# A graph layer on one core: preparation in a hand-written order, the output's bias loaded by type, and an input of the last norm added by TensorE

## The chip, the cores and the metric

The kernel runs on one core of a Trainium2 chip. The metric is the device time of one execution in microseconds; the times below are from three runs, and one further execution was profiled. The engines are named as in the profile: PE (TensorE, the matmuls; PEld its weight loads), DVE (VectorE), ACT (ScalarE), POOL (GpSimd, which also issues the gathers and scatters by index), SP (SyncE, which issues most plain transfers).

## The reference, cut to what matters

One layer of a graph network over N = 3125 nodes of width 256, E = 103125 edges (sorted by destination) and 19 node types. All in float32.

```python
h = layernorm(x)                                   # per row
# graph part: projections with the matrices of the node's own type; four heads of 56
K, Q, V = h @ Wk[type] + bk[type], h @ Wq[type] + bq[type], h @ Wv[type] + bv[type]
e0, e1, e2 = (cos(log(edge_attr[:, i] + 1)[:, None] * w_time + b_time) for i in range(3))
# each edge gives a message from src to dst and one back; q is summed over its heads
att, v = messages(K[src], Q[dst], V[src], e1, e2);  att_i, v_i = messages(K[dst], Q[src], V[dst], e2, e1)
agg = segment_sum([v * segment_softmax(att, dst), e0], dst) + segment_sum([v_i * segment_softmax(att_i, src), e0], src)
y = layernorm(h + concat(agg, agg) @ Wa[type] + ba[type]) * gamma[type] + beta[type]
# mixing part: linear attention over all nodes, 8 heads, phi(u) = elu(u) + 1
k, v, q = phi(h @ wk + bk), h @ wv + bv, phi(h @ wq + bq)
m = (q @ (k.T @ v)) / (q @ sum(k) + 1e-6) @ wo + bo       # per head
X = x + y + m
# mixture of 16 experts, two for each node, and a last norm
z = layernorm(X)
out = X + layernorm(z + experts(z)) * gamma2 + beta2
```

(The kernel sums the two halves of `Wa`, which meet the same `agg`.)

## The kernel before, in words

Rows of 128 nodes make a tile: NT = 25 tiles in the order of the nodes, JS = 43 tiles in the order of the types (a tile has one type, `owner_s[j]`), JT = 64 tiles in the order of the experts.

**Preparation (L193 to L593).** The node tiles lie in `XN`; their norm is taken (bn_stats L424, bn_aggr L425, normalise L430), each tile is transposed into `XNT` (L285, L286) and scattered by type to `xbuf` in memory. For the edges, `dst` is read as `idx` and turned to floats (`nf`); 25 counts over `firsts` (L391) give `row_i`, the line in which each node's edges begin, 25 gathers `er` and 25 counts (L401) the place within it. The nodes are sorted by type (`sorted_rows`) and by number of edges: the degree sort (L468 to L494) makes running sums of 25 x 64 one-hot entries, ranks by matmul (`pr`, L487, L488), and at the end `place_i`. 25 scatters put the node records into `order`, and `ordt` is read back from it (L555). The edge attributes are brought to logarithms in four quarters (L507 to L517, written to `recs`). The weights `w` hold Wk and Wv as they are, and Wq folded from 192 to 56 columns (`fold`, L527 to L529), one type at a time with two buffers. The mixing part's sums over nodes are made in a loop over 25 tiles: keys and values by matmul (`ps_kv`, L573), `k`, `low`, `v` and again `k` by VectorE (L576, L578, L581, L583, with the exponential on ScalarE), and the sum over rows by matmul (`acc`, L585); then `state`. In all of this stage a scheduler decides each engine's order.

**Projection (L716 on, order by hand).** Per type tile: `xr` from `xbuf` and `bias` from `bbuf` by SP (the bias is one row, repeated over 128 partitions; the row's number is loaded into a register first), two transposes, a matmul with the type's weights (L726), `prow` (L734, three buffers), and a scatter of it into `table` (L740) by POOL. The queries and the mixing part of the node tiles, the sums of the two halves of Wa (L753) and, from the ninth tile on, the edge lists (which need `ordt`) are worked in between.

**Edge blocks.** 25 blocks of gathers from `table` and the attention; from 519 to 2038 us of the span. The change does not touch them.

**Output (L916 on, order by hand).** In groups of four type tiles (QUAD): `ar` (the edge sums) and `yr` (the rows of `xbuf`) are loaded two groups ahead by SP, `ar` is transposed one group ahead, and per tile PE adds up three products in `ps_yo`: the bias (L967), which is the type's row picked out of `ba` by a one-hot matrix, and two halves of the weights (L970). VectorE adds the result to `yr` (L974) and takes the moments; one group later ScalarE normalises and POOL scatters the rows to `obuf`. Between the tiles POOL gathers scale rows `Z` and VectorE adds to `X`.

```python
ps = ps_out.tile([P, D], F32, name="ps_yo")
nc.tensor.matmul(ps, sel_s[:, j:j + 1].to_broadcast([T, P]), ba, start=True, stop=False)
```

**Experts and last norm.** After the experts, `ybuf` holds two result rows for each node. They are fetched in parts of LN = 3 tiles (`yb`), PE adds the two by a product with the identity (L1204), VectorE adds the sum to `Z` (L1225), takes the moments (L913, L914), ScalarE normalises from `Z` (L1210), VectorE multiplies by gamma and adds `X` (L1211, L1212), and SP writes the output. Parts are fetched three ahead and summed one ahead.

Of the kernel before, what the change touches and what calls it, by code (L numbers as in the profile page):

```python
# [97 lines left out]
def gnn_mix_moe_kernel(ctx: ExitStack, tc: tile.TileContext, a, out):  # L98
# [97 lines left out]
    e2 = right.enter_context(tc.tile_pool(name="eprep2", bufs=2, side="right"))  # L196
# [19 lines left out]
    turned = first.enter_context(tc.tile_pool(name="turned", bufs=1))  # L216
    normed = ExitStack()
# [18 lines left out]
    for i, k in enumerate(("wq", "wk", "wv")):  # L236
        nc.sync.dma_start(wqkv[:, :, i, :], a[f"L0_mix_{k}"].rearrange("(c p) o -> p c o", p=P))
    wo = mw.tile([P, 2, D], F32, name="wo")
    nc.sync.dma_start(wo, a["L0_mix_wo"].rearrange("(c p) o -> p c o", p=P))
# [7 lines left out]
    nc.vector.tensor_scalar(bq1, bqc, 1.0, None, op0=OP.add)  # L247
# [8 lines left out]

    zp = first.enter_context(tc.tile_pool(name="zero", bufs=1))
    none = ep.tile([P, ROW], F32, name="none")
    nc.gpsimd.memset(none, -1.0)
# [3 lines left out]
    scales = zp.tile([T, 2, DZ], F32, name="scales")  # L263
# [4 lines left out]
    bo = zp.tile([T, D], F32, name="bo")  # L268
    src = a["L0_mix_bo"]
    nc.gpsimd.dma_start(bo, bass.AP(tensor=src.tensor, offset=src.offset, ap=[[0, T], [1, D]]))  # L270
    nc.vector.tensor_tensor(scales[:, 1, :D], scales[:, 1, :D], bo, OP.add)
# [4 lines left out]

    wp = first.enter_context(tc.tile_pool(name="wproj", bufs=1))
    w = wp.tile([P, T, 2, WC], F32, name="w")
# [17 lines left out]

    def sorted_rows(gp, ps_r, pick, K, J):

# [7 lines left out]
        nc.tensor.matmul(total.rearrange("p t e -> p (t e)"), ones, pv, start=True, stop=True)  # L306
        run = gp.tile([P, NT + 1, K], F32, name="run0")
# [59 lines left out]

    nf = ep.tile([P, EW + 1], F32, name="nf")
    nc.vector.tensor_copy(nf, idx)
    kept_ends = nc.gpsimd.dma_start(ends.rearrange("(p r) t -> p (r t)", p=P), nf[:, :EW]).ins  # L370
    with tc.issue_after(kept_ends):
        nc.sync.dma_start(xbuf.rearrange("(t p) d -> p t d", p=P), bc(blank, 1, JS + 1))
    down = ep.tile([P, EW], F32, name="down")
    nc.vector.tensor_tensor(down, nf[:, :EW], nf[:, 1:], OP.is_gt)
    nc.vector.tensor_reduce(bad[:, 0:1], down, AX.X, OP.max)


    ps = ps_c.tile([P, LR, P], F32, name="ps_first")
    for r in range(LR):
        nc.tensor.transpose(ps[:, r, :], nf[:, r * ET:r * ET + 1].to_broadcast([P, P]), ident)  # L380
    firsts = ep.tile([P, LR * P], F32, name="firsts")
    nc.scalar.copy(firsts, ps.rearrange("p r q -> p (r q)"))
    node_i = ep.tile([P, NT], I32, name="node_i")
    nc.gpsimd.iota(node_i, pattern=[[P, NT]], base=0, channel_multiplier=1)
    rec = ep.tile([P, NT, 4], F32, name="rec")
    node = rec[:, :, 0]
    nc.vector.tensor_copy(node, node_i)
    row = ep.tile([P, NT], F32, name="row")
    for t in range(NT):
        junk = e2.tile([P, max(ET, LR * P)], F32, name="junk", bufs=1)  # L390
        nc.vector.tensor_scalar(junk[:, :LR * P], firsts, node[:, t:t + 1], 0.0, op0=OP.is_lt, op1=OP.add,  # L391
                                accum_out=row[:, t:t + 1])
    nc.vector.tensor_scalar(row, row, -1.0, 0.0, op0=OP.add, op1=OP.max)
    row_i = ep.tile([P, NT], I32, name="row_i")
    nc.vector.tensor_copy(row_i, row)
    within = ep.tile([P, NT], F32, name="within")
    for t in range(NT):
        er = e2.tile([P, ET], F32, name="er", bufs=6)
        counted = gather_rows(er, ends, row_i[:, t:t + 1]).ins
        junk = e2.tile([P, max(ET, LR * P)], F32, name="junk", bufs=1)  # L400
        nc.vector.tensor_scalar(junk[:, :ET], er, node[:, t:t + 1], 0.0, op0=OP.is_lt, op1=OP.add,  # L401
                                accum_out=within[:, t:t + 1])


    with tc.tile_pool(name="sort", bufs=1) as gp, tc.tile_pool(name="ps_r", bufs=1, space=PSUM) as ps_r:
        type_f = gp.tile([P, NT], F32, name="type_f")
        nc.vector.tensor_copy(type_f, type_p)
        nc.vector.tensor_scalar(gtype, type_f, 0.0, None, op0=OP.max)
        pick = gp.tile([P, NT, T], F32, name="pick")
        nc.vector.tensor_tensor(pick, bc(type_f, 2, T), bc(seq[:, :T], 1, NT), OP.is_equal)  # L410
        base, own = sorted_rows(gp, ps_r, pick, T, JS)
        row_of(gp, pick, base, T, JS * P, stype_f)
        nc.vector.tensor_copy(stype, stype_f)
        nc.vector.tensor_copy(owner_s, own[0:1, :])
        nc.vector.tensor_scalar(sel_s, own[:T, :], pcol[:T], None, op0=OP.is_equal)


    mv = stats.tile([P, NT, 2], F32, name="mv_x")
    rs = stats.tile([P, NT], F32, name="r_x")
    with tc.tile_pool(name="ps_t", bufs=2, space=PSUM) as ps_t:  # L420
        for g0, gn in groups:
            for t in range(g0, g0 + gn):
                st = stats.tile([P, nc.vector.BN_STATS_DIM], F32, name="s_x", bufs=4)
                nc.vector.bn_stats(st, XN[:, t, :D])  # L424
                nc.vector.bn_aggr(mv[:, t, :], st)  # L425
            gs = slice(g0, g0 + gn)
            nc.scalar.activation(rs[:, gs], mv[:, gs, 1], AF.Sqrt, bias=eps_c)
            nc.vector.reciprocal(rs[:, gs], rs[:, gs])
            for t in range(g0, g0 + gn):
                nc.vector.tensor_scalar(XN[:, t, :D], XN[:, t, :D], mv[:, t, 0:1], rs[:, t:t + 1],  # L430
                                        op0=OP.subtract, op1=OP.mult)
                transposed(XNT[:, :, t * P:(t + 1) * P], XN[:, t, :D], ps_t, "pt")
                with tc.issue_after(counted):
                    scatter_rows(xbuf, stype[:, t:t + 1], XN[:, t, :], "xrows")


    start = ep.tile([P, NT + 1], F32, name="start")
    nc.vector.memset(start[:, NT:], 0.0)
    nc.vector.scalar_tensor_tensor(start[:, :NT], row, float(ET), within, op0=OP.mult, op1=OP.add)
    nc.vector.tensor_copy(rec[:, :, 1], start[:, :NT])  # L440

    shift = ep.tile([P, 2, P], F32, name="shift")
    nc.vector.memset(shift, 0.0)
    nc.vector.tensor_copy(shift[:, 0, :P - 1], ident[:, 1:])
    nc.vector.tensor_copy(shift[:, 1, P - 1:], ident[:, 0:1])
    ps = ps_c.tile([P, NT], F32, name="ps_next")
    nc.tensor.matmul(ps, shift[:, 0, :], start[:, :NT], start=True, stop=False)
    nc.tensor.matmul(ps, shift[:, 1, :], start[:, 1:], start=False, stop=True)
    deg = ep.tile([P, NT], F32, name="deg")
    nc.vector.tensor_tensor(deg, ps, start[:, :NT], OP.subtract)  # L450
    if NP > N:
        nc.vector.tensor_scalar(deg[:, FULL:], deg[:, FULL:], live, None, op0=OP.mult)
# [115 lines left out]
    for v in vs:  # L568
        nc.vector.memset(v[:, :, P:], 1.0)
# [1163 lines left out]
```

## Time and profile before

| | us |
|---|---|
| median of three runs (2707.68 to 2709.11) | 2709.07 |
| the profiled execution: time | 2717.76 |
| the profiled execution: span | 2716.0 |
| PE busy (share of the span) | 2084.6 (77%) |
| DVE busy | 1918.1 (71%) |
| POOL busy | 1497.5 (55%) |
| ACT busy | 1230.2 (45%) |
| mean granted clock of PE | 0.839 |

How to read it: the span runs from the first to the last instruction of the profiled execution, and all places in time below are microseconds from its start. Busy shares are means over stages that have different limits. The granted clock is the share of full speed at which PE was allowed to run; it was 0.50 or 1.00 in most stretches. A line such as "L726 PE MATMUL ps<-w,xT" names the line of the kernel, the engine, the operation, and the tiles that it writes and reads; "x25 | 10.1, 406 | 9.3 <-PE ps_yy L1204" stands for 25 instructions, 10.1 us busy, 406 ns each, and 9.3 us in which the engine stood idle before them, released by PE's `ps_yy` of L1204.

### The profile page before, as it was taken

The numbers are of one execution on the slowest core, as the hardware profiler recorded it, in microseconds if no ns is written. First come the engines' busy times: TensorE is split into PE (matmuls) and PEld (weight loads), VectorE is DVE, ScalarE is ACT, GpSimd is POOL, SyncE is SP. The second block draws the span as 40 slices with busy tenths as digits, with TensorE's granted clock in tenths as the row PEclk, the third lists the DMA queues.
The fourth block names the chain that finished last, engine by engine and source line by source line (L and its number), as shares of the span: only waits on it lengthen the run. The fifth ranks groups of instructions, "written<-read, shape, count | busy, mean of one in ns | idle before, by whom it ended". The sixth has DMA issues, their size and how long they took to land. (4 is left out here: it accounts for less than half of the span.)

```text
span 2716.0 us, 28309 instructions
## 1 busy us (share of the span) xinstructions
PE 2084.6 (77%) x7139; PEld 1274.6 (47%) x7139; DVE 1918.1 (71%) x3769; ACT 1230.2 (45%) x3019; POOL 1497.5 (55%) x1525
## 2 busy tenths in 40 slices
PE   2268665278898898989988888898877853599994
PEld 1034342134555455555554554455554541377773
DVE  7465777377889899999999998999972463122226
ACT  1112222265666666666666566657632350133332
POOL 3531468776777777777777776766613614222210
PEclk7579787677989898999899899898986755699997
DMA  9434567896667666666666766666636561255554
GB/s 282 137 77 129 165 194 226 286 314 183 181 202 202 177 192 192 195 197 193 190 198 202 199 187 178 192 182 188 178 124 204 174 197 66 99 174 173 174 156 146
DMA packets 236151, 496.03 MB, mean 183 GB/s; under 512 B 31509, under 2 KB 148340, under 8 KB 235476
## 3 DMA queue, kind: packets, MB, share of 16 engines
q0 software_dynamic: 88480, 325.71, 40.2%
q1 hardware_dynamic: 139428, 158.87, 20.0%
q10 hardware_dynamic: 8080, 9.59, 1.2%
q8 instruction: 63, 1.03, 0.1%
q14 instruction: 100, 0.82, 0.1%
HBM read 415.68 MB, written 78.37 MB: 182 GB/s over the span
## 5 line engine op out<-in xcount | busy, mean ns | idle before, releaser
L357 POOL DMA_INDIRECT rowt<-table,idx x854 | 999.8, 1171 | 394.6 <-issue 231.3
L1394 PE MATMUL pl<-rowt,ident 128*128 128x448 f32 (+2 forms) x944 | 496.9, 681 | 100.5 <-issue 55.3
L1394 PEld LDWEIGHTS pl<-rowt,ident 128*128 128x128 f32 x944 | 210.3, 234 | 382.2 <-issue 283.8
L1446 PE MATMUL pa<-keep,ident 128*128 128x256 f32 x1708 | 380.6, 380 | 7.0 <-DVE keep L1444 7.0
L1446 PEld LDWEIGHTS pa<-keep,ident 128*128 128x128 f32 x1708 | 325.7, 191 | 73.5 <-issue 27.7
L1359 PE MATMUL ps_u<-wide,turned 49*128 49x448 f32 (+2 forms) x708 | 323.2, 592 | 47.9 <-ACT turned L1352 27.0
L1338 DVE TENSOR_TENSOR rowt<-rowt 128x1260 f32<-128x1260 f32 (+2 forms) x118 | 178.4, 1512 | 140.4 <-DMA rowt<-table,idx 61.7
L1328 ACT ACTIVATE rowt<-rowt,KT 128x60 f32<-128x60 f32 x854 | 216.2, 334 | 20.9 <-DMA rowt<-table,idx 20.0
L1359 PEld LDWEIGHTS ps_u<-wide,turned 49*128 49x128 f32 x708 | 128.0, 194 | 189.7 <-issue 126.0
L351 POOL DMA_INDIRECT ybuf<-y,to_i x64 | 61.4, 960 | 265.0 <-DVE y L1169 224.0
L1352 ACT COPY turned<-pt 42x128 f32<-42x128 f32 (+2 forms) x118 | 30.6, 259 | 386.6 <-PE pt L1350 218.3
L1387 DVE TENSOR_TENSOR rowt<-rowt,qq 128x672 f32<-128x672 f32 (+2 forms) x236 | 197.7, 878 | 4.0
L1361 ACT ACTIVATE half<-ps_u 128x448 f32<-128x448 f32 (+2 forms) x354 | 190.9, 539 | 2.2 <-remote 1.1
L1161 ACT ACTIVATE hT<-ps_h,b 128x128 f32<-128x128 f32 x256 | 94.1, 368 | 213.2 <-PE ps_h L1160 211.5
L1160 PE MATMUL ps_h<-zT,w 128*128 128x128 f32 x1024 | 180.1, 295 | 12.6 <-ACT hT L1161 10.0
L1339 DVE TENSOR_REDUCE KT<-rowt 128x21 f32<-128x1260 f32 (+2 forms) x118 | 178.3, 1511 | 4.1
L1160 PEld LDWEIGHTS ps_h<-zT,w 128*128 128x128 f32 x1024 | 149.8, 192 | 58.2 <-ACT hT L1161 44.0
L1440 DVE TENSOR_TENSOR keep<-keep,both 128x1176 f32<-128x1176 f32 (+2 forms) x118 | 167.0, 1416 | 0.0
L1355 ACT COPY keep<-rowt 128x1344 f32<-128x1344 f32 (+2 forms) x118 | 159.1, 1348 | 13.3 <-PE pa L1446 13.3
L1165 PE MATMUL ps_e<-w,hT 128*128 x512 | 157.6, 390 | 0.0
L1373 PE MATMUL pe<-te,ident 128*128 128x256 f32 x472 | 117.1, 371 | 34.9 <-ACT te L1362 24.4
L1362 ACT ACTIVATE te<-half 128x448 f32<-128x448 f32 (+2 forms) x236 | 139.1, 590 | 7.8 <-ACT half L1361 0.3
(374 smaller groups left out, 3375.6 us busy)
## 6 DMA issues: line engine op xcount, KB each, us to landing
w<-in_L_ffn_w_dram SPq DMA_DIRECT2D x80, 512.0 KB
rowt<-table,idx POOLq DMA_INDIRECT x854
h<-in_L_gnn_Wa_dram SPq DMA_DIRECT2D x19, 512.0 KB
bias<-bbuf SPq DMA_DIRECT2D x43, 220.0 KB
zbuf<-zero SPq DMA_DIRECT2D x1, 8514.0 KB
zr<-zbuf SPq DMA_DIRECT2D x64, 129.0 KB
yb<-ybuf SPq DMA_DIRECT2D x16, 384.0 KB
xbuf<-blank SPq DMA_DIRECT2D x1, 5654.0 KB
```

Of the source, the lines that this page charges most:

```text
L357: return nc.gpsimd.indirect_dma_start(out=dst, out_offset=None, in_=buf[:, :], in_offset=IndirectOffsetOnAxis(ap=idx, axis=0))
L1160: nc.tensor.matmul(ps[:, f, :], w1[:, c, f * P:(f + 1) * P], zT[:, c, :], start=(c == 0), stop=(c == 1))
L1328: nc.scalar.activation(key[:, s, :], key[:, s, :], AF.Square, bias=chk[q]["b"]["k"][:, s0 + s, 1:2])
L1338: nc.vector.tensor_tensor(times, times, bc(rowt[:, :n, :CAP], 2, 3), OP.mult)
L1339: nc.vector.tensor_reduce(b["times"][:, s0:s1, 1::2], times, AX.X, OP.add)
L1355: nc.scalar.copy(keep[:, :n, :PROJ], rowt[:, :n, VC:QC])
L1359: nc.tensor.matmul(ps[:, :n * 2 * TD], lT, wide[:, k, :n * 2 * TD], start=True, stop=True)
L1361: nc.scalar.activation(half[:, :n, :].rearrange("p s j -> p (s j)"), ps[:, :n * 2 * TD], AF.Sin)
L1387: nc.vector.tensor_tensor(to, kt, bc(qq[:, :n, d, :], 2, 3), OP.mult)
L1394: nc.tensor.matmul(pl[:, :n], ident, part[:, :, :, a, :], start=(a == 0), stop=(a == PARTS - 1))
L1440: nc.vector.tensor_tensor(v3, v3, bc(b["both"][:, s0:s1, :3], 3, DK), OP.mult)
L1446: nc.tensor.matmul(b["pa"], ident, keep[:, s, :], start=(s0 + s == 0), stop=(s0 + s == c - 1))
```

## The change

Three edits, in one version.

First, everything from the edges' first counts to `state` stands in one `manual_schedule` block, in which each engine's order is that of the text. SP asks for the mixing weights, the blank of `xbuf`, Wk and Wv ahead of everything else; ScalarE loads the last two edge quarters. The 25 edge counts run in one piece ahead of the type sort; all moments are taken before one square root. A loop over the 25 tiles normalises, transposes and counts, with a key tile (`keys`: the products and VectorE's part for one tile, and the sum of the tile before) behind every second one; the scatters to `xbuf` come behind the loop. The degree sort is a generator (`order_rows`) with 14 steps, behind each of which one `keys()` runs, and every third time one of five folds (four types each instead of one). The scatters to `order` follow, each with a copy of its index column by POOL ahead (`apart`), as do those to `xbuf`.

Second, the output's bias row is loaded by type for each tile (`bas`) and added to `yr` by VectorE (`shift`); the product with `sel_s` goes.

Third, in the last norm `Z` enters the sum on PE as a third product with the identity; the moments and ScalarE read the sum in PSUM. Parts have two tiles instead of three, are fetched four ahead and summed two ahead, with more buffers.

The diff, cut to its core:

```diff
-    ba = wp.tile([T, D], F32, name="ba")
-    nc.scalar.dma_start(ba, a["L0_gnn_ba"])
...
+            bas[j] = op.tile([P, D], F32, name="ba", bufs=2 * QUAD)
+            ks = nc.sync.value_load(owner_s[0:1, j:j + 1], min_val=0, max_val=T - 1)
+            nc.sync.dma_start(bas[j], a["L0_gnn_ba"][bass.ds(ks, 1), :].to_broadcast([P, D]))
+
+        def shift(j):
+            y = yrs[j][:, :D]
+            nc.vector.tensor_tensor(y, y, bas.pop(j), OP.add)
...
             for j in parts[i + 1]:
                 turn(j)
+            for j in range(j0, j1):
+                shift(j)
             if i > 0:
                 write(*groups[i - 1])
             for j in range(j0, j1):
                 kp = nc.tensor.value_load(owner_s[0:1, j:j + 1], min_val=0, max_val=T - 1)
                 ps = ps_out.tile([P, D], F32, name="ps_yo")
-                nc.tensor.matmul(ps, sel_s[:, j:j + 1].to_broadcast([T, P]), ba, start=True, stop=False)
                 agT = agTs.pop(j)
                 for c in range(2):
                     nc.tensor.matmul(ps, agT[:, c, :],
                                      wa[:, bass.ds(kp, 1), c * D:(c + 1) * D].rearrange("p t o -> p (t o)"),
-                                     start=False, stop=(c == 1))
+                                     start=(c == 0), stop=(c == 1))
...
-        with tc.tile_pool(name="fin", bufs=4) as fo, tc.tile_pool(name="ps_fin", bufs=6, space=PSUM) as ps_fin:
+        with tc.tile_pool(name="fin", bufs=6) as fo, tc.tile_pool(name="ps_fin", bufs=8, space=PSUM) as ps_fin:
-            LN = 3
+            LN = 2
...
-                        ps = sums[t] = ps_fin.tile([P, D], F32, name="ps_yy")
+                        ps = sums[t] = ps2[:, t - t0, :]
+                        nc.tensor.matmul(ps, ident, Z[:, t, 0, :D], start=True, stop=False)
                         for k in range(2):
-                            nc.tensor.matmul(ps, ident, ybs[i][:, k, t - t0, :], start=(k == 0), stop=(k == 1))
+                            nc.tensor.matmul(ps, ident, ybs[i][:, k, t - t0, :], start=False, stop=(k == 1))
...
-                        nc.scalar.activation(y, Z[:, t, 0, :D], AF.Identity, bias=ms[:, t:t + 1], scale=rs[:, t:t + 1])
+                        nc.scalar.activation(y, sums.pop(t), AF.Identity, bias=ms[:, t:t + 1], scale=rs[:, t:t + 1])
...
-                        z = Z[:, t, 0, :D]
-                        nc.vector.tensor_tensor(z, z, sums.pop(t), OP.add)
-                        moments(mv, t, z, "f")
+                        moments(mv, t, sums[t], "f")
```

The new order of the preparation, with what it calls (added lines of the diff):

```python
def apart(idx, side):
    at = ep.tile([P, 1], I32, name=f"at_{side}", bufs=3)
    nc.gpsimd.tensor_copy(at, idx)
    return at
...
with tc.manual_schedule():
    ...
    for q in range(2):
        load_edges(q, nc.sync)
    for i, k in enumerate(("wq", "wk", "wv")):
        nc.sync.dma_start(wqkv[:, :, i, :], a[f"L0_mix_{k}"].rearrange("(c p) o -> p c o", p=P))
    nc.sync.dma_start(wo, a["L0_mix_wo"].rearrange("(c p) o -> p c o", p=P))
    nc.sync.dma_start(xbuf.rearrange("(t p) d -> p t d", p=P), bc(blank, 1, JS + 1))
    load_w(w[:, :, :, :PROJ], a["L0_gnn_Wk"], nc.sync)
    load_w(w[:, :, :, PROJ:2 * PROJ], a["L0_gnn_Wv"], nc.sync)
    ...
    def keys():
        t = n_keys[0]
        n_keys[0] += 1
        if t < NTR:
            keys_of(t)        # ps_kv, k, low, v
        if 0 < t <= NTR:
            sum_keys(t - 1)   # the second k, acc

    keep_edges(0)
    load_edges(2, nc.scalar)
    keep_edges(1)
    load_edges(3, nc.scalar)
    with tc.tile_pool(name="ps_t", bufs=2, space=PSUM, side="right") as ps_t:
        for t in range(NT):
            if t + 6 < NT:
                kept_er[t + 6] = er_p.tile([P, ET], F32, name="er")
                gather_rows(kept_er[t + 6], ends, row_i[:, t + 6:t + 7])
            nc.vector.tensor_scalar(XN[:, t, :D], XN[:, t, :D], mv[:, t, 0:1], rs[:, t:t + 1],
                                    op0=OP.subtract, op1=OP.mult)
            transposed(XNT[:, :, t * P:(t + 1) * P], XN[:, t, :D], ps_t, "pt")
            junk = er_p.tile([P, max(ET, LR * P)], F32, name="junk", bufs=1)
            nc.vector.tensor_scalar(junk[:, :ET], kept_er.pop(t), node[:, t:t + 1], 0.0, op0=OP.is_lt, op1=OP.add,
                                    accum_out=within[:, t:t + 1])
            if t % 2 == 1 and t > 2:
                keys()
    for t in range(NT):
        scatter_rows(xbuf, apart(stype[:, t:t + 1], "x"), XN[:, t, :], "xrows")
    ...
    for q in range(2, 4):
        keep_edges(q)
    ...
    for i in range(2):
        load_fold(i)
    ...
    steps = order_rows()
    i = 0
    for s, _ in enumerate(steps):
        if n_keys[0] <= NTR:
            keys()
        if s % 3 == 2 and i < len(folds):
            fold_one(i)
            i += 1
    for t in range(NT):
        scatter_rows(order, apart(place_i[:, t:t + 1], "o"), rec[:, t, :], "order")
    nc.gpsimd.dma_start(ordt, order.rearrange("(t p) c -> p t c", p=P))
    while n_keys[0] <= NTR:
        keys()
    while i < len(folds):
        fold_one(i)
        i += 1
    ...
```

## The prediction

> **What bounds the kernel now.** The page comes first: no engine is full for the whole span. Its two rows of 40 slices (68 us each) show where the changed stages lie: slices 1 to 4 (preparation, then the start of the projection loop), 31 and 32 (output projection behind the edges), and the last one (final norm). The edge blocks between them are untouched.
>
> ```profile
> DVE  7465777377889899999999998999972463122226
> PEclk7579787677989898999899899898986755699997
> ```
>
> Second, the windows, one per stage, for busy time and granted clock (columns: window, length, PE busy, PEld, DVE, ACT, POOL, clock, DMA share, GB/s).
>
> ```profile
> 116.00:147.00 31.00, 13.59 (x16) 4.85 (x17) 24.49 (x71) 6.75 (x11) 2.05 (x3) 0.50 0.41 127
> 147.00:228.00 81.00, 60.12 (x199) 30.55 (x197) 45.41 (x153) 9.58 (x23) 26.34 (x26) 0.89 0.28 58
> 2056.00:2086.00 30.00, 29.95 (x68) 17.63 (x68) 9.56 (x30) 6.07 (x15) 6.71 (x10) 0.50 0.59 180
> 2086.00:2120.00 34.00, 32.15 (x135) 20.22 (x134) 17.03 (x54) 13.17 (x33) 23.03 (x35) 1.00 0.88 269
> 2661.00:2693.00 32.00, 24.37 (x92) 18.17 (x91) 29.29 (x94) 9.70 (x21) 1.41 (x2) 0.92 0.61 206
> ```
>
> The reader sees that from 147 to 228, where 23 of the 25 key tiles run, VectorE is busy 56% of the time; in the output stage TensorE is full at first, at half clock; in the final norm VectorE is full (92%).
>
> Third, the timeline: the two rows that decide when POOL is free, one key tile in the present steady state, and a row of the projection (start, length, what).
>
> ```profile
> 186.16 0.97 POOL L351 DMA_INDIRECT order<-rec,place_i  x1 [0.30 <-issue]
> 190.54 1.62 POOL L555 DMA_DIRECT2D ordt<-order  x1 [3.42 <-issue]
> ...
> 203.10 0.42 DVE L576 TENSOR_TENSOR k<-ps_kv,bkv 128x256 f32<-128x256 f32 x1 [0.25 <-PE ps_kv L573]
> 203.45 1.88 PE L573 MATMUL ps_kv<-wqkv,XNT 128*128 128x512 f32 x4
> 204.60 0.43 DVE L583 SCALAR_TENSOR_TENSOR k<-k,low 128x256 f32<-128x256 f32 x1 [0.54 <-ACT low L579]
> 205.17 0.62 PE L585 MATMUL acc<-v,k 128*128 128x129 f32 x4
> ...
> 252.97 0.62 DVE L734 TENSOR_TENSOR prow<-ps,bias 128x440 f32<-128x440 f32 x1
> ```
>
> `place_i` is written at 154.8, the order scatters run 155 to 187, POOL is free at 192.2; the first table scatter starts at 240.6. So 48 us of slack lie between them. The keys' end (228) and the queries, not the order list, set the projection's start at 237.4. The fourth row of the projection table is made at 252.97.
>
> Fourth, the groups of the two last stages:
>
> ```profile
> L970 PE MATMUL ps_yo<-wa,agT 128*128 x172 | 64.6, 511 | 0.0
> L351 POOL DMA_INDIRECT obuf<-yo,to x43 | 43.0, 999 | 54.1 <-ACT yo L942 41.3 <-issue 8.8 <-POOL to L944 3.5
> L967 PE MATMUL ps_yo<-ba,sel_s 19*128 19x256 f32 x86 | 38.1, 530 | 4.9 <-DVE yr L974 2.9 <-issue 1.9
> ...
> L1204 PE MATMUL ps_yy<-yb,ident 128*128 128x256 f32 x100 | 29.0, 446 | 15.1 <-DVE Z L1225 8.0 <-DMA yb<-ybuf 6.7
> L1225 DVE TENSOR_TENSOR Z<-Z,ps_yy 128x256 f32<-128x256 f32 x25 | 10.1, 406 | 9.3 <-PE ps_yy L1204 9.3
> ```
>
> **Part 1, the hand order.** I follow the one chain that ends in the order list.
>
> Start of the loop over XN: in the new order ScalarE's loads of the edge quarters 2 and 3 stand behind the loads of Wk and Wv (the compiled program has them wait for the lanes of these transfers), and VectorE's `keep_edges(1)` behind those. About 18.6 MB are asked for before that: x 3.2, dst 0.4, edges 1.2, mix weights 1.0, xbuf's blank 5.8, Wk 3.7, half of Wv 1.9, gathers and fills 1.4. Slice 1 moved 282 GB/s: 66 us, and some 6 for a late start, the Ln (1.76) and the reduction (0.77): the loop starts at 72. VectorE's own work before it (25 edge counts of 0.82, 25 moments of 0.6, the type sort of 12) would end at about 63 and hides behind the loads.
>
> The loop: 11 rounds of two tiles and one key tile. In TensorE's order a round is acc 0.71, two transposed tiles 1.06, kv 1.88, together 3.65; then VectorE needs k, low, v and the second k, 1.53, before the next acc; with 0.2 of handing over 5.4 us, at half clock 7.3+1.7 = 9.0. Today a key tile costs 2.2, because the scheduler puts kv ahead of the acc that waits. One round at half clock and ten at full are 63, the four tiles without keys 4: end at 139. `keep_edges` 2 and 3 (0.34, 1.76, 0.77 each and one table load of 1.28) take 7: 146.
>
> The order sort: 14 steps, each followed by one `keys()`. Its own VectorE work (running sums of 1.5 to 2.0, three ranks of 2.0) hides behind acc and kv; a round is 0.71+1.88+1.53+0.2 = 4.3, at half clock 7.0. The four pairs of rank matmuls (a full one 1.9) stand ahead of kv and add 6. I take four rounds at half clock, since TensorE has just been idle for 7 us, and ten at full: 28+43+6 = 77. `place_i` comes at 223 instead of 155.
>
> Then POOL: each order scatter now has its index copy ahead, as L944 has before the scatters of the output (0.20+0.28+0.98 = 1.47): 25 take 36.8, and the ordt transfer 5.0 (3.42 idle, 1.62). The table scatters are queued behind it on POOL; `prow` has three buffers, so the fourth waits for the first scatter (copy and issue 1.5, landing estimated at 2). 223+45.3 = 268.3 against 252.97: **+15.3**. The other path, over the last key, fold, state, checks and queries (some 15.5 from `place_i` to the first product, 9 of them as now between 228 and 237.4; then 15.5 to the fourth row, as now from 237.4 to 252.97), would give 254, so it is hidden. The five larger folds instead of 19 save some 6 us of VectorE, beside waits; they are worth nothing here, and would count only if the loop were VectorE's. The xbuf scatters (25 of 1.47, done by about 155) hide under the order sort. No engine is full in the projection loop (TensorE 12.5 of 20 us, VectorE 13.6), but its tiles follow each other in order, so I pass the delay on whole.
>
> Ends: all rounds at full clock and the loads done 6 us earlier put `place_i` at 202 and the term at -6; half of the loop and all of the order rounds at half clock give +40.
>
> A page bears on this: the Trainium skill, "TensorE: Matmul & The Clock Gate", section "What's actually happening", says that full clock comes after one window of about 3.4 us of sustained activity. By that rule one half-clock round is enough after the pause, and the term is about +7, not +15. The row 2056 to 2086 speaks against it: busy 29.95 of 30 us, clock 0.50. By that row, seven half-clock rounds, it would be +23. Four lies between.
>
> **Part 2, the bias by type.** Removed: 43 L967, 38.1 us of TensorE. Added per tile: a register load and a broadcast transfer on SP, and a VectorE addition of 0.42 (18 us in all, beside VectorE at 32 to 50%). In the projection loop the same pair follows an xr load at 1.6 us a tile; with ar and yr (0.95 together) I get 2.15 a tile, 8.6 a group of four. TensorE at half clock needs 4 x 2.01 + 1.71 = 9.75 a group instead of 14.35; POOL 4 x 1.47 + 2 x 1.29 = 8.5. So all three come close to each other. The second group's transposes stand ahead of the first product, so that it waits for eight tiles' loads: 2043.4+17.2+2+1.7 = 2064 instead of 2056.7; the four products then take 8 instead of 12.6, and the first scatter comes at 2076 instead of 2073.5. From it POOL needs 94 us (43 x 1.47 and 24 x 1.29), with 0 to 10 us of gaps (today 14): end at 2170 to 2180 against 2181.7. I take **-6**; ends -12 (no gaps) and +2 (SP sets the pace).
>
> **Part 3, the last norm.** VectorE loses L1225, 25 x 0.41, of 1.87 a tile: 1.45 left. TensorE gains a third matmul: today 12 records take 3.38 at full clock, so six are 1.69 a tile, and TensorE becomes the limit. From 2658.5, four us at half clock and then 142 records of 0.27: 2701; the last part's norm adds 5, 2706, against 2710 today. **-3.5**; ends -7 (VectorE's own sum) and +2 (the clock falls: 4 records took 2.16 from 2693.66, at half clock, so six take 3.2).
>
> Sum: +15.3-6-3.5 = +5.8 on the profiled execution of 2717.76 (span 2716.0): 2723.6. It lay 8.7 above the median of 2709.07, so I forecast 2715.
>
> **Rivals.** *Faster.* The clock is full from the first rounds and the loads land earlier: the term of part 1 is -6 to 0, and with -9 and -5 for the rest the time is 2689 to 2700. For it: 0.89 from 147 to 228 with TensorE only 74% busy. Against it: 0.50 up to 147.
> *Slower by the clock.* Half of the loop and all order rounds at half clock: +40-9, some 2740, reached if the pause drops the clock and the rounds (74% busy) do not raise it. It decides from about three half-clock rounds on.
> *Part 2 does not do what it says.* SP's 2.15 a tile sets the pace behind a late start, and instead of -6 it costs 2 to 5: 2723 to 2726.
>
> **How the numbers follow.** About 0.2%, 5.4 us, is what a measurement here can tell from no change. The forecast (2706 to 2722) has 0.42, of which 0.15 lies within 0.2% and 0.27 above; faster 0.30; slower by the clock 0.18; part 2 failing 0.10. That gives faster 0.30, same 0.15, slower 0.55. The range 2690 to 2748 leaves out a third of the faster case and half of the slow one's upper part.
>
> **What would show it.** Right: `place_i` between 210 and 235, POOL's order scatters behind it, prow waiting on POOL, rounds of 4.3 to 7 us with kv behind acc. Wrong: `place_i` before 205, or the table's fourth row before 253; the first product after the edges before 2060; L1204 not continuous in the last 50 us.

## The result, and the profile after

| | us |
|---|---|
| before, median of four runs beside the changed kernel (2707.68 to 2725.18) | 2709.09 |
| after, median of four runs (2734.04 to 2757.26) | 2739.77 |
| ratio after to before, 95% interval | 1.0123 [1.0082, 1.0163] |
| profiled execution after: time / span | 2741.94 / 2739.9 |

The changed kernel is slower. The forecast was 2715; the time lies 25 above it and inside the range. The stages, cut at events that both traces have (profiled executions):

| stretch | before | after | difference | predicted |
|---|---|---|---|---|
| start to the first query gather | 519.0 | 538.8 | +19.8 | +15.3 |
| edge blocks | 1518.0 | 1516.9 | -1.1 | 0 |
| end of the edges to the last obuf scatter | 139.9 | 152.4 | +12.5 | -6 |
| to the last ybuf scatter (gate, experts) | 475.7 | 475.9 | +0.2 | 0 |
| last norm | 63.4 | 55.9 | -7.5 | -3.5 |
| span | 2716.0 | 2739.9 | +23.9 | +5.8 |

So part 1 was about as dear as worked out, part 3 brought twice what was worked out, and part 2 has the wrong sign. The page of the changed kernel first: VectorE's busy tenths and the granted clock in 40 slices, here of 68.5 us.

```profile
DVE  7464677457888999999989998999963574122225
...
PEclk9988787668989998999999999999986855599998
```

In the first three slices the clock is 9, 9 and 8 tenths, where it was 7, 5 and 7, while VectorE's digits are 7, 4, 6, as before. The windows (columns as in the prediction) name the stretch of the loop and `keep_edges`, that of the order sort, two of the output and one of the last norm.

```profile
80.00:147.00 67.00, 41.73 (x133) 19.81 (x132) 31.57 (x116) 18.10 (x41) 33.36 (x45) 0.89 0.23 69
147.00:223.00 76.00, 50.72 (x139) 23.57 (x140) 49.61 (x130) 8.86 (x18) 19.24 (x27) 0.85 0.26 83
2083.00:2113.00 30.00, 17.27 (x59) 12.52 (x60) 13.54 (x43) 8.78 (x20) 9.02 (x13) 0.74 0.72 215
2113.00:2143.00 30.00, 15.32 (x60) 11.35 (x59) 17.00 (x56) 8.33 (x22) 18.16 (x27) 0.83 0.77 256
2690.00:2722.00 32.00, 32.00 (x144) 27.68 (x142) 25.04 (x89) 10.02 (x26) 0.98 (x2) 0.96 0.73 239
```

In the first two the clock is 0.89 and 0.85, PE is busy 62% and 67%, VectorE 47% and 65%: no engine is full, and the clock is well above half. In the output (third and fourth) PE is busy 58% and 51%, where it was full before, at 215 to 256 GB/s. In the last row PE is full, 32.00 of 32. The timeline shows why nothing is full in the order sort: one key tile.

```profile
173.23 0.43 DVE L505 TENSOR_TENSOR k<-ps_kv,bkv 128x256 f32<-128x256 f32 x1 [0.72 <-PE ps_kv L502]
...
173.90 0.42 DVE L510 TENSOR_TENSOR v<-ps_kv,bkv 128x256 f32<-128x256 f32 x1
...
174.24 0.41 DVE L517 SCALAR_TENSOR_TENSOR k<-k,low 128x256 f32<-128x256 f32 x1
...
174.71 0.71 PE L519 MATMUL acc<-v,k 128*128 128x129 f32 x4 [1.51 <-DVE k L517]
...
175.25 1.88 PE L502 MATMUL ps_kv<-wqkv,XNT 128*128 128x512 f32 x4
...
177.17 0.42 DVE L505 TENSOR_TENSOR k<-ps_kv,bkv 128x256 f32<-128x256 f32 x1 [0.79 <-PE ps_kv L502]
```

VectorE's first operation on the tile ends at 173.66 and the second k, that of the tile before, at 174.65; only then PE starts acc (idle 1.51), and only behind acc comes the next `ps_kv`, for which VectorE waits in its turn (0.79, and 0.72 ahead of the tile shown). This round takes 3.94 us (173.23 to 177.17); others, with a longer step of the sort or partly at half clock, take up to 5.6. Then the queue of POOL:

```profile
258.60 0.62 DVE L830 TENSOR_TENSOR prow<-ps,bias 128x440 f32<-128x440 f32 x1 [8.85 <-DMA table<-prow,to]
...
268.55 0.98 POOL L354 DMA_INDIRECT order<-rec,at_o  x1 [0.28 <-POOL at_o L426]
...
274.77 1.61 POOL L666 DMA_DIRECT2D ordt<-order  x1 [5.24 <-issue]
...
281.43 0.62 DVE L830 TENSOR_TENSOR prow<-ps,bias 128x440 f32<-128x440 f32 x1 [7.32 <-DMA table<-prow,to]
```

The last order scatter is at 268.55 and `ordt` at 274.77; table scatters come in between, and `prow` waits for them in four places. The fourth row is made at 258.60. For the output and the norm, the groups of their stretches:

```profile
L1072 PE MATMUL ps_yo<-wa,agT 128*128 x172 | 56.1, 492 | 5.0 <-DVE yr L1076 2.3 <-issue 1.8 <-DVE yr L1028 0.9
L354 POOL DMA_INDIRECT obuf<-yo,to x42 | 42.1, 1003 | 65.3 <-ACT yo L1043 49.2 <-issue 12.5 <-POOL to L1045 3.3
...
L286 PE MATMUL ps_at<-ident,ar 128*128 128x128 f32 x86 | 18.9, 323 | 58.3 <-DMA ar<-abuf 50.9 <-issue 3.8 <-ACT agT L287 3.6
```

PE's transposes wait 50.9 us for `ar`, and POOL's scatters 49.2 for ScalarE's rows (41.3 before), which stand behind it. Before, the transposes had waited 5.3:

```profile
L285 PE MATMUL ps_at<-ident,ar 128*128 128x128 f32 x86 | 17.1, 345 | 14.3 <-DMA gam<-in_L_ffn_gamma_dram 8.7 <-DMA ar<-abuf 5.3
```

And the last norm after:

```profile
L1308 PE MATMUL ps_yy<-yb,ident 128*128 128x256 f32 x100 | 27.1, 393 | 7.9 <-DMA yb<-ybuf 7.9
...
L1007 DVE BATCH_NORM_STATS2 s_f<-ps_yy 128x6 f32<-128x256 f32 x25 | 10.6, 425 | 11.0 <-PE ps_yy L1308 11.0
```

In the last norm VectorE's statistics wait for PE, which has become the limit, as predicted.

### The profile page after: what moved, and what is told of

Same layout as the page of the kernel before. It is cut to its first block, busy times and chain, and to the rows that moved or that the text cites. A ratio compares the mean times of both kernels' runs of the same rounds, so it can differ in the third digit from the quotient of the medians.

```text
span 2739.9 us, 28531 instructions
## 1 busy us (share of the span) xinstructions
PE 2055.6 (75%) x7103; PEld 1270.1 (46%) x7103; DVE 1924.9 (70%) x3750; ACT 1229.6 (45%) x3020; POOL 1538.6 (56%) x1577
## 5 line engine op out<-in xcount | busy, mean ns | idle before, releaser
L360 POOL DMA_INDIRECT rowt<-table,idx x854 | 1022.2, 1197 | 367.2 <-issue 229.9
L1465 ACT ACTIVATE te<-half 128x448 f32<-128x448 f32 (+2 forms) x236 | 139.1, 590 | 7.5
```

What stands on the lines that cost most here:

```text
L360: return nc.gpsimd.indirect_dma_start(out=dst, out_offset=None, in_=buf[:, :], in_offset=IndirectOffsetOnAxis(ap=idx, axis=0))
```

## The experiments

They ran in three groups, each beside runs of the kernel before on its own chip (22, 19 and 22 runs): its median was 2663.9, 2721.0 and 2663.0 us there. Ratios are taken against these. The first group has the three parts alone and the row on ScalarE's queue; the second the products ahead, the loads on POOL's queue, six buffers, and one row; the third the fixed row, all rows resident, and the two kernels of all parts. Stretches are compared in the profiles, of one execution each.

### The parts one by one

Part 1 alone: the diff without its second and third part.

> Only the hand order of the preparation; output and last norm as before. Theory: the late order list costs what stands between the two profiles at the first query gather, 538.8 - 519.0 = 20 us; so 2709 + 19 to 20 = some 2729, place_i at 221 to 223. Rival: the parts hang together (shifted memory or a shifted clock), and the order alone costs under 10 or over 30 us.

Measured: 2712.31 us, ratio 1.0164 [1.0131, 1.0196]. `place_i` 223.7, first query gather 542.5, the same places as in the changed kernel (221.6, 538.8); output 138.0, last norm 63.4, as before the change.

Part 2 alone:

```diff
+            bas[j] = op.tile([P, D], F32, name="ba", bufs=2 * QUAD)
+            ks = nc.sync.value_load(owner_s[0:1, j:j + 1], min_val=0, max_val=T - 1)
+            nc.sync.dma_start(bas[j], a["L0_gnn_ba"][bass.ds(ks, 1), :].to_broadcast([P, D]))
...
-                nc.tensor.matmul(ps, sel_s[:, j:j + 1].to_broadcast([T, P]), ba, start=True, stop=False)
```

> Only the output's bias loaded by type. Theory: SP's queue becomes the pace of the output stage; the stage between the edges' end and the last output scatter grows from 139.9 to 152 us, as in the changed kernel (2055.7 to 2208.1), so some 2709 + 12 = 2721, and the loads of the last tile come about 117 us after the first. Rival: the stage was slow there only because the preparation had left something behind; then it is -6 as predicted, some 2703.

Measured: 2672.27 us, ratio 1.0041 [1.0016, 1.0067]; from the end of the edges to the last obuf scatter 144.8 us, the first product of the weights 26.4 behind the end of the edges (139.1 and 21.0 in the next kernel, which has the old bias, on the same chip). That is 5.7 us more, not the 12 of the first comparison.

Part 3 alone:

```diff
+                        nc.tensor.matmul(ps, ident, Z[:, t, 0, :D], start=True, stop=False)
...
-                        nc.vector.tensor_tensor(z, z, sums.pop(t), OP.add)
-                        moments(mv, t, z, "f")
+                        moments(mv, t, sums[t], "f")
```

> Only the last norm's sum on TensorE. Theory: from the last ybuf scatter to the end 55.9 instead of 63.4 us as between the two profiles, so 2709 - 7.5 = some 2701.5. Rival: TensorE at 1.69 us a tile is the limit, as in the prediction, and the gain is 3.5: 2705.5.

Measured: 2652.08 us, ratio 0.9954 [0.9931, 0.9978]; last norm 57.7 us instead of 63.4. So parts 1 and 2 cost time each by itself, and part 3 saves. (By the ratios part 2 costs 11 us and part 3 saves 12, twice what their stages show; the intervals, 4 to 18 and 6 to 18, reach down to about that.) Part 1 costs 44 us on this chip by the ratio, 56 up to the first query gather in the traces, and some 20 in the first comparison: its own order takes the same time in both (`place_i` at 223.7 and 221.6), but the scheduler's order that it replaces is quicker here: the kernels of this group without part 1 reach the first query gather at 486 to 487 us, against 519.0 in the trace of before.

### Part 1: the lockstep, the loads, the buffers

The next tile's products ahead of the sum of the tile before:

```diff
+            if t == 0:
+                products_of(0)
+            if t + 1 < NTR:
+                products_of(t + 1)
             if t < NTR:
                 keys_of(t)
```

> Part 1 alone, with the keys and values of the next tile asked of TensorE ahead of the sum (acc) of the tile before. My theory: a round is long because TensorE takes acc, which waits for VectorE's second k, ahead of the next kv. Then the rounds of the loop fall from 4.7 us to about 3.7 (TensorE's own 3.65), those of the order sort from 4.4 to about 3.4, place_i comes some 20 us earlier (about 204 instead of 223.7), the first query gather 15 to 20 us earlier (about 525 instead of 542.5). Rival: VectorE's own work (steps of the order sort of 1.5 to 2.0 with the 1.53 of a key tile) sets the rounds; then place_i moves by less than 8 us.

Measured: 2695.89 us, ratio to before 0.9898 [0.9851, 0.9945]. `place_i` came at 179.0, the first query gather at 492.6: some 45 us earlier than in the changed kernel, more than twice what was expected. The timeline of its order sort:

```profile
145.08 0.42 DVE L509 TENSOR_TENSOR k<-ps_kv,bkv 128x256 f32<-128x256 f32 x1
...
146.08 0.43 DVE L521 SCALAR_TENSOR_TENSOR k<-k,low 128x256 f32<-128x256 f32 x1
...
146.56 0.71 PE L523 MATMUL acc<-v,k 128*128 128x129 f32 x4 [0.71 <-DVE k L521]
...
147.11 1.88 PE L504 MATMUL ps_kv<-wqkv,XNT 128*128 128x512 f32 x4
...
148.16 0.41 DVE L509 TENSOR_TENSOR k<-ps_kv,bkv 128x256 f32<-128x256 f32 x1
```

acc still waits for k (0.71), but `ps_kv` of the next tile was asked for long before, so that VectorE goes on at 148.16 without a wait, 3.08 us after the tile before. In the loop a round fell from a mean of 5.23 us (11 key tiles from 88.15 to 140.46) to 3.11 (87.96 to 119.03). The window of its order sort:

```profile
147.00:180.00 33.00, 28.48 (x94) 14.68 (x93) 30.60 (x85) 3.75 (x9) 10.95 (x15) 0.95 0.22 70
```

VectorE is busy 30.6 of 33 us: now it is the bound. The lockstep of PE and VectorE was the whole cost of part 1 on this chip, and more. The expected 3.65 per round in the loop, the sum of PE's durations, was too long: at its best a round took 2.66. There (from 92.15 us on) the trace has acc with 0.61, the transposes with 0.66 and kv with 1.88, and each starts some 0.17 before the listed end of the one ahead.

The loads of edge quarters 2 and 3 and the writes of `recs` on POOL's queue:

```diff
-        load_edges(2, nc.scalar)
+        load_edges(2, nc.gpsimd)
...
-        load_edges(3, nc.scalar)
+        load_edges(3, nc.gpsimd)
...
-        nc.scalar.dma_start(recs[...], rc)
+        nc.gpsimd.dma_start(recs[...], rc)
```

> Part 1 alone, with the loads of edge quarters 2 and 3, and the writes of recs, on POOL's queue instead of ScalarE's. My theory: ScalarE stood at these requests behind the loads of Wk and Wv, and VectorE behind ScalarE; then the loop over XN starts at about 70 instead of 79, and place_i moves by the same 9 us (about 215). Rival: the memory's traffic itself sets the start (18.6 MB asked for ahead of it); then the loop starts within 3 us of 79, and the first query gather stays at 542 or so.

Measured: 2739.55 us, ratio to before 1.0058 [1.0031, 1.0085]; `place_i` 221.6, first query gather 534.9. The first key tile came at 74.69 instead of 88.15: the loads by ScalarE had held up the loop, by more than expected. But VectorE lost it again:

```profile
148.11 0.19 DVE L603 COPY rec<-stype_f 128x25 f32<-128x25 f32 x1
159.23 0.18 DVE L605 COPY kind<-rec 128x25 f32<-128x25 f32 x1 [10.93 <-DMA recs<-rc]
```

By the profile the sort's first tile waits 10.93 us for the write of `recs`, which now stands on POOL's queue, behind the scatters to `xbuf`: the last of these starts at 154.14, the writes at 155.13. The gain at one end of the chain became a wait at the other; how early the write would have to be was not tried.

Six buffers for `prow`:

```diff
-            prow = mp.tile([P, WC], F32, name="prow", bufs=3)
+            prow = mp.tile([P, WC], F32, name="prow", bufs=6)
```

> Part 1 alone, with six buffers for prow instead of three. My theory: the rows wait because each buffer is freed by a table scatter, which stands behind the order scatters on POOL. With six, VectorE's waits on the table scatters (28 us in six places in the changed kernel) fall below 12, and the first query gather comes 8 to 13 us earlier than 542.5. Rival: POOL's queue sets the pace, not the buffers: the seventh row waits instead of the fourth, and the first query gather moves by less than 4 us.

Measured: 2727.09 us, ratio to before 1.0032 [0.9994, 1.007]; from `place_i` to the first query gather 305.9 us, 317.2 in the changed kernel and 318.8 with part 1 alone. What VectorE's `prow` waits for between 225 and 345 us: in the changed kernel

```profile
DVE prow L830 <- DMA table<-prow,to: 24.5, 4, 8.8
```

and with six buffers nothing of the table: its longest wait is 3.6 us for `bias`. So the buffers were the wait. It is worth 7 to 13 us: the five kernels with three buffers and the hand order took 313.3 and 313.6 us (the two on this chip) to 318.8 from `place_i` to the first query gather.

### Part 2: the product, the register load, the transfer

One row, loaded once, for all tiles (the bias of each type's own is left out):

```diff
-            bas[j] = op.tile([P, D], F32, name="ba", bufs=2 * QUAD)
-            ks = nc.sync.value_load(owner_s[0:1, j:j + 1], min_val=0, max_val=T - 1)
-            nc.sync.dma_start(bas[j], a["L0_gnn_ba"][bass.ds(ks, 1), :].to_broadcast([P, D]))
+            bas[j] = row0
```

> Part 2 alone, without the choice of the row: the bias of type 0 is loaded once and added to every tile, so SP has neither the register load nor the row transfer, while TensorE stays without the product L967 and VectorE has the added addition. My theory: SP's pace was what part 2 cost; then from the end of the edges to the last obuf scatter it takes 130 to 136 us (139.1 with the old bias, 144.8 with part 2), the first product comes about 21 us behind the end of the edges (26.4 with part 2), and the time is 3 to 9 us below the kernel before. Rival: POOL and the memory set this stage's length; then it takes 138 to 141 us, the time is within 3 us of the kernel before, and the product L967 had cost nothing.

Measured: 2698.46 us, ratio 0.9892 [0.9845, 0.9939]; the stage 125.8 us, the first product 22.1 behind the end of the edges. Before it was 139.9, and 134.2, 141.5 and 140.3 in the three kernels with the old bias on this chip. So the product L967 had cost some 8 to 16 us of this stage, and the load by type takes that back. (The time fell by more, 29 us by the ratio; the profile doesn't say where the rest is, and before itself spread from 2698 to 2736 here.) Which half of the load? The transfer kept, the register load left out, with row 0 for every tile:

```diff
-            ks = nc.sync.value_load(owner_s[0:1, j:j + 1], min_val=0, max_val=T - 1)
-            nc.sync.dma_start(bas[j], a["L0_gnn_ba"][bass.ds(ks, 1), :].to_broadcast([P, D]))
+            nc.sync.dma_start(bas[j], a["L0_gnn_ba"][0:1, :].to_broadcast([P, D]))
```

> Part 2 alone, with the row transfer kept for each tile but always of row 0, so that the choice of the row (the register load on SP) is left out. From the end of the edges to the last obuf scatter it took 139.9 us before, 144.8 with part 2, 125.8 with one resident row. Theory A, the register load holds SP (0.85 of its 2.1 us a tile): the stage takes 126 to 131 us. Theory B, the transfer itself costs, by its place in SP's queue and its traffic on the DMA engines: the stage takes 138 to 145 us.

Measured: 2676.65 us, ratio 1.0054 [1.0027, 1.0081]; the stage 150.0 us, above even what theory B expected, the first product 28.8 behind the end of the edges. With all rows resident, on the same chip, the stage takes 123.7 (below). So leaving out the register load alone gains nothing; the stage is long while each tile has its transfer. In the list of waits of this stage (total, times, longest), PE's transposes still wait for `ar`:

```profile
PE ps_at L285 <- DMA ar<-abuf: 45.8, 23, 4.3
```

How often SP asks for `ar` shows what holds it up. From the first request to the last a tile took SP 2.28 us before, 2.75 in the changed kernel, 2.57 with part 2 alone, 2.69 with the fixed row, and 1.86 with the rows resident. In the changed kernel and with part 2 alone the trace names what SP waits for in only 17 of 116 and 23 of 108 us; for the rest, as far as the trace shows, SP is at its own instructions, the register load among them. With the fixed row it names 60 of 113, 41 of them for transfers that have not landed. So with the register load SP's queue is the pace, and without it SP waits for the transfers and is no faster.

The DMA queues of the stage show what was added. SP's queue (packets, MB, share of 16 engines' time) before, over 140 us:

```profile
q1 hardware_dynamic: 12416, 11.32, 27.4%
```

with part 2 alone, over 145 us:

```profile
q1 hardware_dynamic: 18608, 16.96, 42.3%
```

and with the fixed row, over 150 us:

```profile
q1 hardware_dynamic: 18608, 16.96, 48.2%
```

43 transfers of 128 KB add 6192 packets and 5.6 MB. They take 42.3% of 145 less 27.4% of 140, 23 us of all 16 engines, and with the fixed row 34, in a stage whose DMA share was 0.58 to 0.87 already in each window of its first 110 us. How much of the delay is this traffic and how much the requests on SP, no run separates. In the two traces of this chip that list it, an `ar` landed a median of 5.2 us after its request in the changed kernel (run again, below) and 4.4 with the rows resident: it is asked for late more than it lands late.

Would another queue do? The register load and the row transfer by ScalarE:

```diff
-            ks = nc.sync.value_load(owner_s[0:1, j:j + 1], min_val=0, max_val=T - 1)
-            nc.sync.dma_start(bas[j], ...)
+            ks = nc.scalar.value_load(owner_s[0:1, j:j + 1], min_val=0, max_val=T - 1)
+            nc.scalar.dma_start(bas[j], ...)
```

> The bias by type alone, with the register load and the row's transfer on ScalarE's queue in place of SP's. Theory (SP's queue is the pace, 2.7 us a tile): SP has 0.95 us a tile again, the output stage is bound by POOL, and the kernel gains 6 to 12 against before: 2697 to 2703. Rival (the transfers themselves, 43 repeated rows of 131 KB, fill the DMA engines or land late): no better than on SP, 2715 to 2725. Third: ScalarE's own work waits behind the issues, in between.

Measured: 2677.61 us, ratio 1.0062 [1.0037, 1.0088]; the stage 154.6 us. Its waits:

```profile
ACT agT L286 <- DMA ba<-in_L_gnn_ba_dram: 44.1, 8, 7.6
PE ps_at L285 <- ACT agT L286: 40.7, 9, 5.9
```

ScalarE's copies now stand behind the row transfers, and PE behind ScalarE. The same bytes on another queue cost no less, but since ScalarE's waits come on top, this doesn't tell the traffic from the place in a queue.

All rows resident: one transfer ahead of the stage repeats the 19 rows over the partitions, and VectorE loads the type's number for each tile.

```diff
+    bar = wp.tile([P, T, D], F32, name="bar")
+    nc.scalar.dma_start(bar, bass.AP(tensor=src.tensor, offset=src.offset, ap=[[0, P], [D, T], [1, D]]))
...
+            kv = nc.vector.value_load(owner_s[0:1, j:j + 1], min_val=0, max_val=T - 1)
+            nc.vector.tensor_tensor(y, y, bar[:, bass.ds(kv, 1), :].rearrange("p t o -> p (t o)"), OP.add)
```

> Part 2 alone, with the rows of all 19 types repeated over the partitions by one transfer ahead of the stage; for each tile VectorE loads the type's number and adds that row from SBUF. SP is as before the change, TensorE has no L967. If SP's pace was the cost of part 2, the stage takes 125 to 132 us as with one resident row, and the time is 8 to 15 us below the kernel before. Rival: the register load now holds VectorE (43 of some 0.85 us, in front of the addition to yr), and the stage takes 135 to 142 us, with no gain over before.

Measured: 2650.91 us, ratio 0.9959 [0.994, 0.9977]; the stage 123.7 us. POOL's scatters in it:

```profile
L351 POOL DMA_INDIRECT obuf<-yo,to x43 | 43.8, 1019 | 35.1 <-ACT yo L948 23.3 <-POOL to L950 9.7 <-issue 1.9
```

The first scatter is at 2034.5, the last at 2127.6, and POOL's last gather of `Z` ends at 2132.4: 97.9 us for what the prediction had worked out as POOL's 94. Of the 23.3 us for ScalarE's rows 21.0 lie ahead of the first scatter. With the transfers gone, POOL sets this stage's length, as the prediction had it. VectorE's register loads cost little: 14.9 us stand as "issue" ahead of the additions.

### All together

The changed kernel again, beside the last one:

> The changed kernel as it is, beside the mended one and the kernel before on one chip. If the three parts add, its ratio is the sum of the three alone: +0.3 to 1.6% for part 1 by chip, +0.4% for part 2, -0.5% for part 3. Rival: it lies above 1.02, and the parts cost more together than alone.

Measured: 2721.34 us, ratio 1.0229 [1.0195, 1.0264]. `place_i` 223.5, first query gather 539.0, output 148.3, last norm 56.9. The parts alone add up to 1.64 + 0.41 - 0.46 = 1.6%, with an uncertainty of some 0.5; together they cost 2.3%, on another chip. The profiles put only a few us of the rest anywhere (the output takes 148.3, against 144.8 for part 2 alone), so it stays open whether the parts cost more together.

The changed kernel with three repairs (products ahead, six `prow` buffers, rows resident):

> All three parts, with the next tile's key products issued ahead of the sum, six prow buffers, and the bias rows resident in SBUF. If each repair keeps its worth: place_i at about 179, first query gather at about 481 (492.6 with the products ahead, less 11 for the prow buffers), the output stage 126 to 132 us, the last norm 7 us shorter than before: a span of about 2655 to 2665, 50 us below the kernel before where that takes 2716, some 20 where it takes 2670. Rival: the earlier projection meets waits on the xbuf scatters or the weights, and the first query gather comes no earlier than 490.

Measured: 2643.72 us, ratio to before 0.9929 [0.9902, 0.9956]; `place_i` 174.5, first query gather 481.3, output 126.5, last norm 56.7, span 2641.0, 14 us below the lower end of what was expected. It is faster than both kernels: 19 us below before and 78 below the changed one on this chip.

## Why the prediction was right or wrong

**Part 1, +15.3 worked out, +19.8 in the trace.** The chain held: loop, `keep_edges`, order sort, `place_i` (223 worked out, 221.6 measured), POOL, `prow`. Two of its errors cancel: the loop began at 79 instead of 72, and 11 rounds took 5.2 us each on average. The order sort took 72 instead of 77. The last step, "268.3 against 252.97", was wrong in its form. Its 2 us of landing stand on no row (a table scatter took a median of 4.7 to 5.3 us in the eight traces that list it), and table scatters slipped in between the order scatters, the fourth row came at 258.60, only 5.6 late, and the rows behind it waited another 15.6 for the table in three places; by the eighth row (291.93 against 271.89) the delay was 20. What the prediction had in front of it and passed by is what the kernel with the products ahead showed: it said that the scheduler "puts kv ahead of the acc that waits" and gave the price of not doing so, but as a fact of the new order, not as the one cause that a line of it would mend. And the size of the term depends on the chip: in the first and third group the scheduler's order is quicker up to here by 31 to 34 us than in the trace of before, and in the first the same hand order costs 44.

**The clock.** One round of the loop and four of the order sort were taken at half clock, 9 and 28 us, between a rule and a row. The windows have 0.89 from 80 to 147 and 0.85 from 147 to 223. If the clock was 0.50 or 1.00 throughout, that is 15 and 23 us at half: nearly the same sum, in other places (three rounds of the loop went to half clock in the middle of steady work). So the choice of four came out in its sum, by luck more than by a rule, and neither of its two sources was a good guide. The row 2056 to 2086 (0.50 at full PE) would have given 49 us in the sort. By the page "TensorE: Matmul & The Clock Gate" of the Trainium skill (section "What's actually happening"), one window of about 3.4 us of sustained activity would have been enough behind the pause; here the clock was 0.50 from 152 to 156 us with PE busy 3.19 of the 4, and 0.54 from 156 to 160 with 3.30 (whether that is sustained in the page's sense, the trace doesn't say). The rival "slower by the clock" named 2740, which is the time that came, for a reason that did not: at half clock throughout the order sort the window would have 0.50, not 0.85. Its mechanism is refuted, and the agreement is chance.

**Part 2, -6 worked out, +12.5 in the trace (+5.7 alone): the step that failed.** The prediction gave SP 2.15 us a tile for its requests, saw SP, TensorE and POOL close to each other, and let POOL's 94 us end the stage. The 2.15 was right at first (2.0 to 2.3 a tile for the first seven with part 2 alone) and too short over the stage: 2.57 there, and 2.75 in the changed kernel. So SP, not POOL, was the pace, and POOL's scatters ran 107.7 and 114.2 us from the first to the last. Beyond 2 us of landing at the start, which stand on no row (an `ar` took a median of 4.3 to 5.2 where a trace lists it), the transfers themselves had no price, though the row shown for 2086 to 2120 had a DMA share of 0.88 at 269 GB/s; with the fixed row SP waited for them, and the stage was no shorter. All in all the new pair cost more than the product that it replaces: 134 to 142 us with the product, 124 to 127 with neither, 145 to 152 with part 2, 150 with the transfer and no register load. The start of the stage was forecast well (the first product +7.3, measured +7.6, against L967 before), but the register load is not what makes it late: without it the first product came 28.8 behind the edges, and 27.3 in the changed kernel. The rival "Part 2 does not do what it says" had the sign and SP as the pace, with a cost of 2 to 5 us. PE at half clock did not last: it had 0.74 and 0.83 in the two windows shown, half idle.

**Part 3, -3.5 worked out, -7.5 in the trace (-5.7 alone).** The mechanism was right: VectorE loses L1225 and TensorE becomes the limit, full in the last row. The term that was too long is "six are 1.69 a tile", half of the old trace's 12 records in 3.38 us. A longer run of the same trace, 42 records in 9.67 us from 2664.84 on, would have given 0.23 each and 1.38 a tile. In the changed kernel a tile took 1.29 us of PE, and the gain reached the end given for VectorE's own sum, -7.

## What to carry to other kernels

An order written by hand for two engines that hand work to each other should issue the next tile's first step ahead of this tile's last: here one such change moved `place_i` by some 45 us and turned a loss into a gain. Before a product is replaced by a transfer, follow the queue that asks for it over the whole stage, and read the stage's DMA share: here SP needed 2.57 to 2.75 us a tile where 2.15 had been worked out, at a share of 0.6 to 0.9, and the pair cost more than a product that kept TensorE full. A table that is loaded once and picked by an engine kept the gain. A wait that is taken away at one queue should be followed through to the last one: the loads moved to POOL came back as a wait on the write of `recs`.

## What the runs showed of the hardware

**The bias product and the clock.** Columns as before; the stretch 2060 to 2070, some 25 us behind the end of the edges, before the change:

```profile
2060.00:2070.00 10.00, 10.00 (x22) 5.93 (x23) 3.64 (x11) 0.00 (x0) 0.00 (x0) 0.50 0.58 173
```

and with one resident row, without L967:

```profile
2060.00:2070.00 10.00, 10.00 (x50) 8.11 (x49) 8.08 (x26) 3.45 (x9) 1.20 (x2) 0.90 0.80 228
```

TensorE is busy without a gap in both; the clock is 0.50 in the first and 0.90 in the second. Before the change it rose only after 2080, some 25 us of uninterrupted work later. By the page cited above one busy window of 3.4 us would have been enough; this row of before disagrees. It is tempting to blame the 19-row products L967 that stand in between, but the other runs don't bear that out. In the 30 us from 20 us behind the end of the edges on, the mean clock was 0.50 to 0.52 in three kernels with L967 and 0.73 to 0.79 in three others with it; in the eight without it was 0.73 to 0.86. Windows of 10 us in this stage with TensorE busy throughout and a clock of 0.50 occur only with L967, but L967 does not always bring them. What keeps the clock down is open.

**The same row is no cheaper.** If all that SP's queue took more than before is put on the added 6192 packets, reading row 0 each time took 34 us of 16 engines, 88 ns a packet on each, against 59 with rows by type; two profiles of two chips, so the order of the two is not firm.

**Chips differ in some stretches only.** The scheduler's preparation reached the first `prow` at 239.2 and 239.5 us in the first comparison and on the chip of the second group, and at 202.6 to 205.2 in five kernels on the chips of the first and third group, while the hand order without the repair to its rounds gave 232.6 to 239.0 on all of them. From the last obuf scatter to the first expert product every kernel took 175 to 178 us in the former and 155 to 157 in the latter. (Whether the first comparison ran on the chip of the second group is not known.) The cause is open; the profile names no releaser for part of those waits.
